# Twenty-four chains of taps in groups of three in the tail's linear attention

## The chip, the core and the metric

The kernel runs on one core of one Trainium2 chip. The core has five engines, each with an instruction queue of its own that it works through in order: PE (TensorE, matrix products), DVE (VectorE), ACT (ScalarE), POOL (GpSimd) and SP (SyncE, which here only issues transfers). Engines wait for each other by semaphores. The metric is the device time of one execution in microseconds (us); smaller is better.

## The reference

Four images of 256 channels and 64 x 64 pixels, float32, go through four layers. Each one normalises its input by groups, computes, and adds its result to what came in:

```python
x = x + layer0(gn(x))   # 1x1 conv, deformable sampling, feed-forward
x = x + layer1(gn(x))   # linear attention
x = x + layer2(gn(x))   # 3x3 convolution with binarised weights
x = x + layer3(gn(x))   # softmax attention over a max-pooled image
```

The change concerns layer 1, and one buffer of layer 2. Layer 1, cut to what matters:

```python
qkv = relu(conv2d(x, qkv_w, 'SAME') * qkv_bn_scale + qkv_bn_bias)  # 768 channels
agg = conv2d(qkv, agg_dw_w, [(2, 2), (2, 2)], groups=C3) + agg_dw_b  # 5x5, each channel alone
agg = conv2d(agg, agg_pw_w, 'SAME', groups=C3) + agg_pw_b            # one factor per channel
ms = concatenate([qkv, agg], axis=1)                                 # 64 heads of 24 channels
q, k, v = split(ms.reshape(B, -1, 24, H * W), 3, axis=2); q = relu(q); k = relu(k)
vk = einsum('bhdn,bhen->bhde', v, k)
out = einsum('bhde,bhen->bhdn', vk, q)
denom = einsum('bhe,bhen->bhn', k.sum(-1), q)
out = relu(bn(conv2d(out / (denom + EPS), proj_w)))
```

The 5 x 5 convolution of each channel by itself is what the "taps" are: 25 products with a factor per channel, summed, for each of 768 channels and 4096 pixels.

## The kernel before

A tile of work holds 128 channels (the partitions) by pixels. The 768 channels of qkv are six such tiles, two each of q, k and v. An image is cut into eight blocks of 512 pixels (NB), and for the taps into four pieces of 16 rows, 1024 pixels (NCH). So one image needs 6 x 4 = 24 **chains of taps**, each of 25 instructions of 128 x 1024 elements.

Layers overlap between images. Generators hand out work piece by piece, each piece with a cost, and `beside` advances several of them by shares of their stated totals. Most of the run is bound by the gathers of layer 0's sampling on GpSimd, with the other layers of earlier images beside it. When the fourth image has been sampled, the **tail** begins (`self.alone` is set in `run`). Its first stage runs three works in the share of 0 to 1: the feed-forward of image 3 (0 to 0.27), the linear attention of image 3 (0.27 to 1, with the total LAST), and layers 2 and 3 of image 2, called `rest` (0.27 to 1.05). The instructions of PE, DVE, ACT and POOL stand in this stage in the order in which the program emits them; SP's do not. The second stage runs layer 2 of image 3, conv(3), beside what is left of `rest`, in an order that a scheduler chooses. Layer 3 of image 3 ends the run.

Linear attention is `layer1`. `rows` produces: for three pairs of tiles, (k, v), (k, v) and (q, q), it multiplies each block by the weights (L824), and ScalarE writes the result into a padded buffer of 20 rows (`pad0` for the first of the pair, `pad1` for the second; `padded` clears the edges with memsets on DVE, L459). In the tail `room(3)` gives each of the two names four buffers. When a piece of 16 rows is complete, it goes to `ready`, and `chains` hands out its two chains in order.

A chain is done in one of two ways. `aggregate` runs it on DVE: `depthwise` multiplies and adds in one instruction per tap, the first at L180, the others at L178, into an accumulator in PSUM. `products` runs it on two engines: ScalarE multiplies a tap into one of three buffers named m (L196), and GpSimd adds that to the sum in SBUF (L200); it takes 28 steps for 25 taps, because its adds trail its products by up to two steps.

Around the taps stands `step`, which is called with `chains=True` once for each tap on DVE in the tail. At every second tap it takes one item from the list `later` and emits it; at count 6 of 8 it advances `rows` once; and it advances the chains on ScalarE and GpSimd. `later` holds the uses of finished chains: the outer products of k and v (`outer`: transposes, a copy on ScalarE, a product), their combination (`summed`), and for the q pieces the `output` (denominators L924, inverse L928 and L929 on DVE, heads, projection L946, residual). They are `staged`: each item holds the next link of up to three or more uses, so that one engine's link is a step ahead of the next engine's.

Nine of the chains (`ASIDE`) run on ScalarE and GpSimd, taken by `others` from the same sequence as DVE takes its own; `due` grows with each tap by `ASIDE * 28 / (6 * NCH - ASIDE) / 25` = 9 x 28 / 15 / 25 = 0.672, and each whole unit advances them by a step. These run across the ends of DVE's chains, independently of them. What is left of them after DVE's fifteenth chain is drained, then what is left in `later`.

Layer 2 is `layer2`. For each of eight blocks `normed` takes a buffer `xp`, clears its edges (DVE, L1049), loads ten rows (SP, L1052) and normalises them (ScalarE, L1053); `parts` forms sums and differences from it (L1041, on GpSimd in the tail), and PE multiplies them (L1090). The results are added to the residual on DVE (L1070 to L1074). In the tail `xp` has two buffers, so the next block can be loaded while the current one is read. Layer 3's softmax takes for each 128 pixels the products L1190, the largest element (DVE, L1191), the exponential (ScalarE, L1196), transposes, and the product L1208.

Of the kernel before, what the change touches and what calls it, by code (L numbers as in the profile page):

```python
# [38 lines left out]

CONVOLVE, OFFSETS, BINARY = NB * 9 + 26, 60, 62  # L40
FEED = NB * 40 + 8
LINEAR, LAST, ASIDE = 938, 592, 9
STEPS = 900
CONV, SECOND = NB * 22.5 + 11, 568
EPS_BN = 1e-5
# [26 lines left out]
class Net:  # L72
# [684 lines left out]
    def layer1(self, n, st, st2):  # L757
# [3 lines left out]
        with tc.tile_pool(name=f"la{n}", bufs=1, side="right") as sp, \  # L761
# [10 lines left out]
            ld = sp.tile([P, 4, 2, 32], F32, name="ld")  # L772
            nc.vector.memset(ld, 0.0)

            later, count, aside, due = [], 0, None, 0
            alone = self.alone
            room = lambda bufs, more=1: bufs + more * alone

            def step(cost, chains=False):


                nonlocal count, due
                count += chains
                if later and (not alone or count % 2 or not chains):
                    later.pop(0)()
                if chains:
                    if count % 8 == 6 if alone else count in LEADS:
                        next(made, None)
                    if aside:
                        due += ASIDE * 28 / (6 * NCH - ASIDE) / 25  # L790
                        while due > 1:
                            next(aside, None)
                            due -= 1
                return cost


# [12 lines left out]
            def rows():  # L809


                for t, tiles in enumerate(((2, 4), (3, 5), (0, 1))):
                    new = lambda c: [self.padded(bp, 1, 20, 2, c, f"pad{i}", bufs=room(3)) for i in range(2)]
                    pads = {0: new(0)}
                    for b in range(NB):
                        c, h = divmod(b, 2)
                        x = self.block(bp, self.x3_d[n], b, "xr")
                        if h and c + 1 < NCH:
                            pads[c + 1] = new(c + 1)
                        got = []  # L820
                        for i, m in enumerate(tiles):
                            ps = self.ps()
                            for k in range(KT):
                                nc.tensor.matmul(ps, qw[:, k, m * P:(m + 1) * P], x[:, k], start=k == 0, stop=k == KT - 1)  # L824
                            if alone:
                                yield
                            bn = {"bias": qb[:, m:m + 1], "scale": self.vec("qkv_s", m)}
                            dst = {j: p[i][:, 0] for j, p in pads.items()}
                            if t < 2:
                                v = bp.tile([P, 512], F32, name="v", tag=f"v{i}")  # L830
                                added = {} if i else {"accum_out": ks[t][:, 0, b:b + 1]}
                                nc.scalar.activation(v, ps, AF.Relu, **bn, **added)
                                self.spread(dst, rw(v), b, 2)
                                got.append(v)
                            else:
                                self.spread(dst, None, b, 2, lambda own: nc.scalar.activation(own, rw(ps), AF.Relu, **bn))  # L836
                            if i:
                                if got:
                                    outer(t, 0, *got, t == 0 and b == 0, False)
                                for j in [c - 1] * (b > 0 and not h) + [c] * (b == NB - 1):  # L840
                                    ready.append((t, tiles, j, [p[:, 0] for p in pads.pop(j)]))
                            if not alone:
                                yield
# [163 lines left out]
                    yield step(3)  # L1007
                return args

            def others():  # L1010

                for _ in range(ASIDE):
                    while not (args := next(every)):
                        yield
                    *args, more = args
                    yield from products(*args, **more)

            if alone:
                aside, number = others(), ASIDE
            while number < 6 * NCH:  # L1020
                count = 0 if not alone and number % 2 == 0 else count
                *args, more = yield from chain()
                yield from aggregate(*args, **more)
                number += 1
            if aside:
                for _ in aside:
                    pass
            while later:
                yield step(2 if alone else 4)

# [1 line left out]
    def layer2(self, n, st, st3, side="left"):  # L1032
# [3 lines left out]
        with tc.tile_pool(name=f"ca{n}", bufs=1, side=side) as sp, \  # L1036
                tc.tile_pool(name=f"cb{n}", bufs=2, side=side) as bp:
            w = sp.tile([P, KT, 3, 4, C], F32, name="w2")
            nc.sync.dma_start(w, self.w2_d)
            sc, bi = yield from self.groupnorm(sp, st, "g2")  # L1040
            add = lambda out, a, b, op=ALU.add: (nc.gpsimd if self.alone else nc.vector).tensor_tensor(out, a, b, op)  # L1041

            def normed(b):

                lo, hi = max(8 * b - 1, 0), min(8 * b + 9, H)
                xp = bp.tile([P, KT, 10, W + 2], F32, name="xp", bufs=1 + self.alone)
                for v in [xp[:, :, :, 0:1], xp[:, :, :, W + 1:]] + [xp[:, :, 0:1, 1:W + 1]] * (b == 0) \
                        + [xp[:, :, 9:10, 1:W + 1]] * (b == NB - 1):
                    nc.vector.memset(v, 0.0)  # L1049
                for k in range(KT):  # L1050
                    v = xp[:, k, lo - 8 * b + 1:hi - 8 * b + 1, 1:W + 1]
                    nc.sync.dma_start(v, self.x4_d[n][:, k, lo * W:hi * W].rearrange("p (r w) -> p r w", w=W))  # L1052
                    nc.scalar.activation(v, v, AF.Identity, bias=bi[:, k:k + 1], scale=sc[:, k:k + 1])  # L1053
                d = xp.rearrange("p k r (x d) -> p k r x d", d=2)
                return [d[:, :, :, c // 2:c // 2 + W // 2, c % 2] for c in range(4)]

            def parts(d):
                v = bp.tile([P, 4, KT, 10, W // 2], F32, name="xd")
                add(v[:, 0], d[0], d[2], ALU.subtract)
                add(v[:, 1], d[1], d[3], ALU.subtract)  # L1060
                yield
                add(v[:, 2], d[1], d[2])
                add(v[:, 3], d[2], d[1], ALU.subtract)
                yield v

            def leave(b, m, half, ps, xv):

                y = xv[:, m].rearrange("p (q d) -> p d q", d=2)
                if not half:
                    nc.vector.tensor_tensor(y, y, ps, ALU.add)  # L1070
                    return
                nc.vector.tensor_tensor(y, y, ps[:, 0:1].to_broadcast([P, 2, 256]), ALU.add)
                nc.vector.tensor_tensor(y[:, 0], y[:, 0], ps[:, 1], ALU.add)
                nc.vector.tensor_tensor(y[:, 1], y[:, 1], ps[:, 1], ALU.subtract)  # L1074
                if m == KT - 1:
                    self.stats(st3, xv, b)
                    nc.sync.dma_start(self.x5_d[n][:, :, b * 512:(b + 1) * 512], xv)

            before, made = [], []
            for d in parts(normed(0)):  # L1080
                yield 2
            for b in range(NB):
                v, xv = d, self.block(bp, self.x4_d[n], b, "x4")
                ahead = iter(())
                for m in range(KT):
                    for half in range(2):
                        ps = self.long().rearrange("p (e q) -> p e q", e=2)
                        for i in range(12):
                            e, k, t = i // 6, i // 3 % 2, i % 3
                            nc.tensor.matmul(ps[:, e], w[:, k, t, 2 * half + e, m * P:(m + 1) * P], v[:, 2 * half + e, k, t:t + 8],  # L1090
                                             start=i % 6 == 0, stop=i % 6 == 5)
                            if i % 3 == 2:
                                if before and (i > 5 or not self.alone):
                                    before.pop()()
                                if i == 5 and b + 1 < NB:
                                    if not (m or half):
                                        ahead = parts(normed(b + 1))
                                    elif half:
                                        d = next(ahead)
                                yield 1.4  # L1100
                        before.append(partial(leave, b, m, half, ps, xv))
            before.pop()()
# [286 lines left out]
```

## Time and profile before

| | us |
|---|---|
| median of 3 runs | 8705.34 |
| lowest and highest | 8691.91, 8707.14 |
| the profiled execution | 8769.03 |
| its span | 8767.3 |
| the tail, from the end of the gathers | about 1577 (7190 to 8767) |
| first to last tap on DVE in the tail | 702.4 (7551.6 to 8254.0) |

Durations below come from the profiled execution, which took 0.7% longer than the median. Over its whole span the engines were busy as follows (us and share, then the number of instructions):

```profile
PE 5927.3 (68%) x35776; PEld 3524.6 (40%) x35776; DVE 4790.2 (55%) x6020; ACT 3564.8 (41%) x10792; POOL 4995.0 (57%) x4894
```

In the table of slices each digit is the busy share of a fortieth of the span, 219 us, in tenths:

```profile
DVE  5344442443366667324776675127766762588723
ACT  2333333234433433344444443444444442456414
POOL 2666666556666666666665556666655560487410
```

The tail is the last seven digits. The chains of taps lie in the sixth- to third-last of them. A row of the table of groups reads: line, engine, operation, output and inputs, shapes, number, then busy us and mean ns of one, then the idle time of the engine just before them and what ended it.

### The profile page before, as it was taken

To read this page: it belongs to the slowest core of one execution; us is meant where nothing else is said; L and a number is where in the kernel's file an instruction comes from. 1 tells how busy PE (TensorE), PEld (TensorE's weight loads), DVE (VectorE), ACT (ScalarE), POOL (GpSimd) and SP (SyncE) were. 2 spreads that over 40 slices of the span, in tenths; PEclk is the share of its full clock that TensorE was granted. 3 is DMA by queue.
4 is the path that set the end of the run, shared out by engine and by line. 5 is a ranking of instruction groups with operands and counts; after the bars stand their busy time and mean duration, and the time that the engine had idled before them with its cause. 6 is when DMAs were issued, how large, how long until landed. Compare 5 with 4: busy or idle time off the path is not lost.

```text
span 8767.3 us, 99783 instructions
## 1 busy us (share of the span) xinstructions
PE 5927.3 (68%) x35776; PEld 3524.6 (40%) x35776; DVE 4790.2 (55%) x6020; ACT 3564.8 (41%) x10792; POOL 4995.0 (57%) x4894
## 2 busy tenths in 40 slices
PE   4454554448744546688876676888766768987899
PEld 2222222223322322335644443345544433664476
DVE  5344442443366667324776675127766762588723
ACT  2333333234433433344444443444444442456414
POOL 2666666556666666666665556666655560487410
PEclk7666666669866667799987787999878879987899
DMA  6454554454433334444443344444433342220131
GB/s 171 129 157 123 144 150 117 119 146 142 153 107 108 105 109 125 135 130 141 135 133 106 110 115 141 141 133 139 139 105 109 111 118 95 77 68 30 44 96 53
DMA packets 744383, 1031.75 MB, mean 118 GB/s; under 512 B 354128, under 2 KB 459984, under 8 KB 742352
## 3 DMA queue, kind: packets, MB, share of 16 engines
q0 software_dynamic: 221184, 604.27, 24.1%
q1 hardware_dynamic: 522704, 421.10, 16.3%
q8 instruction: 283, 4.64, 0.2%
q14 instruction: 212, 1.74, 0.1%
HBM read 856.39 MB, written 168.61 MB: 117 GB/s over the span
## 4 chain that ended last, share of the span: by engine, by line
PE 42%; another core or an unknown queue 18%; DVE 16%; ACT 13%; issue 8%; POOL 2%; DMA 1%; SPq 0%; ACTq 0%; DVEq 0%; POOLq 0%
DVE agg L178 9%; PE acc L603 6%; PE ps L739 5%; ACT wm L588 5%; PE ps L1090 5%; PE ps L749 5%; PE ps L824 3%; PE ps L946 2%; PE ps L1208 2%; PE s L1190 2%; PE po L636 2%; ACT dT L623 2%; ACT at L608 1%; POOL av L200 1%
## 5 line engine op out<-in xcount | busy, mean ns | idle before, releaser
L596 POOL DMA_INDIRECT g<-tab,sl x4608 | 4401.8, 955 | 2848.3 <-issue 1184.1
L178 DVE SCALAR_TENSOR_TENSOR agg<-pad,vec,agg 128x1024 f32<-128x1024 f32 x2257 | 2904.0, 1287 | 63.3
L603 PE MATMUL acc<-g,wm 128*32 128x128 f32 x18432 | 1018.1, 339 | 2033.0 <-ACT at L608 1573.1
L603 PEld LDWEIGHTS acc<-g,wm 128*32 128x32 f32 x18432 | 562.9, 130 | 2532.2 <-ACT at L608 1785.6
L588 ACT ACTIVATE wm<-sl,con 128x48 f32<-128x48 f32 x6144 | 1486.9, 364 | 25.5 <-remote 12.0
L1090 PE MATMUL ps<-xd,w 128*128 128x256 f32 x3072 | 745.9, 395 | 28.6 <-issue 19.1
L623 ACT COPY dT<-dp 64x128 f32<-64x128 f32 x1152 | 296.3, 257 | 972.9 <-remote 475.5
L1090 PEld LDWEIGHTS ps<-xd,w 128*128 128x128 f32 x3072 | 594.4, 199 | 144.4 <-issue 61.1
L608 ACT COPY at<-acc 128x256 f32<-128x256 f32 x576 | 214.4, 372 | 774.5 <-remote 670.6
L739 PE MATMUL ps<-x2f,f 128*128 128x512 f32 x1024 | 506.6, 643 | 11.8 <-DVE hm L724 7.7
L824 PE MATMUL ps<-xr,qw 128*128 128x512 f32 x768 | 469.2, 741 | 19.5 <-issue 7.4
L724 DVE SCALAR_TENSOR_TENSOR hm<-ps,vec,lk 128x512 f32<-128x512 f32 x256 | 190.6, 749 | 518.7 <-ACT lk L741 391.6
L749 PE MATMUL ps<-hm,f 128*128 128x512 f32 x1024 | 463.5, 601 | 0.0
L200 POOL TENSOR_TENSOR av<-av,m 128x1024 f32<-128x1024 f32 x144 | 342.9, 2382 | 110.8 <-ACT m L196 102.0
L741 ACT ACTIVATE lk<-ps,low 128x512 f32<-128x512 f32 x256 | 174.3, 687 | 529.2 <-PE ps L739 401.5
L1041 POOL TENSOR_TENSOR xd<-xp 128x640 f32<-128x640 f32 x64 | 79.5, 1270 | 522.7 <-ACT xp L1053 421.9
L878 ACT COPY kt<-pt 128x512 f32<-128x512 f32 x256 | 149.2, 583 | 532.5 <-remote 255.6
L636 PE MATMUL po<-dT,ow 128*128 128x288 f32 x1024 | 328.7, 468 | 49.5 <-issue 14.1
L1208 PE MATMUL ps<-gt,pT 128*128 128x129 f32 x2048 | 316.8, 316 | 44.2 <-ACT pT L1204 34.8
L613 PE MATMUL dp<-ident,at 128*128 128x128 f32 x1152 | 288.2, 340 | 83.0 <-ACT dT L623 55.6
L1208 PEld LDWEIGHTS ps<-gt,pT 128*128 128x128 f32 x2048 | 299.1, 227 | 96.4 <-ACT pT L1204 45.8
L1190 PE MATMUL s<-ph,th 128*128 128x512 f32 x512 | 287.6, 673 | 46.0 <-ACT pad L836 12.6
(243 smaller groups left out, 7700.2 us busy)
## 6 DMA issues: line engine op xcount, KB each, us to landing
g<-tab,sl POOLq DMA_INDIRECT x4608
x<-x SPq DMA_DIRECT2D x128, 512.0 KB
xr<-x SPq DMA_DIRECT2D x96, 512.0 KB
tab<-xo SPq DMA_DIRECT2D x192, 128.0 KB
x<-in_x SPq DMA_DIRECT2D x32, 512.0 KB
y<-yc SPq DMA_DIRECT2D x32, 512.0 KB
yb<-y SPq DMA_DIRECT2D x64, 256.0 KB
x<-yb SPq DMA_DIRECT2D x64, 256.0 KB
```

Of the source, the lines that this page charges most:

```text
L178: nc.vector.scalar_tensor_tensor(to, s, wt, acc, ALU.mult, ALU.add)
L588: nc.scalar.activation(wm[:, :, :, o], blocks[b][:, r:r + WR, G:], AF.Copy, scale=self.con("own")[:, o:o + 1])
L596: nc.gpsimd.indirect_dma_start(out=g[:, i, :], out_offset=None, in_=table, in_offset=bass.IndirectOffsetOnAxis(ap=sl.bitcast(I32)[:, r, i: ...
L603: nc.tensor.matmul(acc[32 * i:32 * i + 32, :], wm[:, r4, 4 * i + 2 * x:4 * i + 2 * x + 2, :], g[:, i, x * P:(x + 1) * P], start=x == 0, st ...
L623: nc.scalar.copy(dT[b][hs, :, r:r + UR], dp[u][hs, :, :, s, :].rearrange("p v g o -> p g v o"))
L636: nc.tensor.matmul(po[m][:, 0:BR * OB], self.ow[:, k, m * P:(m + 1) * P], dT[b][:, k].rearrange("p r o -> p (r o)"), start=k == 0, stop=k ...
L739: nc.tensor.matmul(ps, f1[:, k, m * P:(m + 1) * P], x2[:, k], start=k == 0, stop=k == KT - 1)
L749: nc.tensor.matmul(ps, f2[:, k, m * P:(m + 1) * P], hm[:, k], start=k == 0, stop=k == 4 * KT - 1)
L824: nc.tensor.matmul(ps, qw[:, k, m * P:(m + 1) * P], x[:, k], start=k == 0, stop=k == KT - 1)
L1090: nc.tensor.matmul(ps[:, e], w[:, k, t, 2 * half + e, m * P:(m + 1) * P], v[:, 2 * half + e, k, t:t + 8], start=i % 6 == 0, stop=i % 6 == 5)
L1190: nc.tensor.matmul(s[i], tv[:, 4 * b + j], ph[:, i * 512:(i + 1) * 512], start=True, stop=True)
L1208: nc.tensor.matmul(ps[:, 0:P + 1], pT[:, m], gt[:, m], start=m == 0, stop=m == 7)
```

## The change

The fixed number ASIDE and the running count `due` go. In the tail the loop now takes three chains at a time: the first goes to DVE; the second, `slow`, to ScalarE and GpSimd; then the third to DVE. Every second tap of the two DVE chains (an odd `count`) advances the slow one by one step; after the third chain what is left of the slow one is drained. Eight such groups make 16 chains on DVE and 8 on ScalarE and GpSimd, in the place of 15 and 9. The total LAST, by which `beside` paces the layer, becomes 624. In the tail `pad1` gets a fifth buffer, and `xp` of layer 2 has one buffer in the place of two, in both stages of the tail. The staging of the uses stays as it is, and nothing changes ahead of the tail.

```diff
-LINEAR, LAST, ASIDE = 938, 592, 9
+LINEAR, LAST = 938, 624
...
-            later, count, aside, due = [], 0, None, 0
+            later, count, aside = [], 0, None
...
-                    if aside:
-                        due += ASIDE * 28 / (6 * NCH - ASIDE) / 25
-                        while due > 1:
-                            next(aside, None)
-                            due -= 1
+                    if count % 2 and aside:
+                        next(aside, None)
...
-                    new = lambda c: [self.padded(bp, 1, 20, 2, c, f"pad{i}", bufs=room(3)) for i in range(2)]
+                    new = lambda c: [self.padded(bp, 1, 20, 2, c, f"pad{i}", bufs=room(3) + (alone and i)) for i in range(2)]
...
-            def others():
-
-                for _ in range(ASIDE):
-                    while not (args := next(every)):
-                        yield
-                    *args, more = args
-                    yield from products(*args, **more)
-
-            if alone:
-                aside, number = others(), ASIDE
             while number < 6 * NCH:
                 count = 0 if not alone and number % 2 == 0 else count
                 *args, more = yield from chain()
-                yield from aggregate(*args, **more)
-                number += 1
-            if aside:
-                for _ in aside:
-                    pass
+                if alone:
+
+                    *slow, smore = yield from chain()
+                    aside = products(*slow, **smore)
+                    yield from aggregate(*args, **more)
+                    *args, more = yield from chain()
+                    yield from aggregate(*args, **more)
+                    for _ in aside:
+                        pass
+                    number += 3
+                else:
+                    yield from aggregate(*args, **more)
+                    number += 1
...
-                xp = bp.tile([P, KT, 10, W + 2], F32, name="xp", bufs=1 + self.alone)
+                xp = bp.tile([P, KT, 10, W + 2], F32, name="xp", bufs=1)
```

More of the change, by code (lines that the diff above doesn't have):

```diff
@@ L779, in step @@
             def step(cost, chains=False):
-                nonlocal count, due
+                nonlocal count
                 count += chains
```

## The prediction

> **What bounds the kernel now.** I read the page's slices first: the tail, from about 7190 us, has no gathers on GpSimd (POOL) any more, and the digit of DVE rises to 8. Then I cut the tail into windows by what runs there, and read busy time in each (the columns are window, its length, busy us and instructions of PE, PEld, DVE, ACT and POOL, granted clock, DMA share, GB/s).
>
> ```profile
> 7551.00:7815.00 264.00, 242.87 (x1165) 196.02 (x1163) 232.97 (x273) 170.44 (x228) 237.30 (x113) 0.98 0.23 68
> 7815.00:8254.00 439.00, 321.08 (x1154) 195.12 (x1154) 397.60 (x442) 267.85 (x369) 308.23 (x129) 0.80 0.13 41
> 8254.00:8358.00 104.00, 93.07 (x321) 50.57 (x320) 43.01 (x69) 30.51 (x50) 0.00 (x0) 0.89 0.16 54
> 8358.00:8520.00 162.00, 155.66 (x714) 134.17 (x715) 46.10 (x112) 28.14 (x38) 39.55 (x32) 0.95 0.38 112
> ```
>
> The first two rows are the chains of taps beside the binarised convolution of image 2, then beside its softmax: DVE is 88% and 91% busy, 630.6 of 703 us. The third is the drain, the outputs that are left after the last tap, where PE is 89% busy. The fourth, conv(3), is PE at 96%. Next, the groups of the window of the chains, and what DVE waits for in it (us in total, times, longest).
>
> ```profile
> L178 DVE SCALAR_TENSOR_TENSOR agg<-pad,vec,agg 128x1024 f32<-128x1024 f32 x345 | 443.3, 1285 | 8.3
> L200 POOL TENSOR_TENSOR av<-av,m 128x1024 f32<-128x1024 f32 x144 | 342.9, 2382 | 110.8 <-ACT m L196 102.0
> L200 POOL TENSOR_TENSOR ak<-ak,m 128x1024 f32<-128x1024 f32 x72 | 171.3, 2379 | 41.6 <-ACT m L196 37.0
> L1041 POOL TENSOR_TENSOR xd<-xp 128x640 f32<-128x640 f32 x26 | 32.5, 1272 | 0.0
> L196 ACT ACTIVATE m<-pad,vec 128x1024 f32<-128x1024 f32 x216 | 246.6, 1158 | 63.0 <-POOL av L200 43.7 <-POOL ak L200 19.0
> ```
> ```profile
> DVE rden L1211 <- PE ps L1208: 10.7, 5, 4.9
> DVE x L1072 <- PE ps L1090: 10.4, 2, 7.6
> DVE mx L1191 <- PE s L1190: 9.6, 9, 3.7
> DVE pad L459 <- ACT m L196: 9.2, 1, 9.2
> ```
>
> Taps alone are 443.3 us of DVE here. Its longest wait inside the chains is the 9.2 us of L459: the memset of a fourth pad buffer stood until ScalarE had read the old contents. All DVE waits over 0.3 us between first and last tap come to 58 us. Last, the chain of waits from 7551 to 8358 goes through the taps most, but through GpSimd's adds for 22.8%:
>
> ```profile
> by line: DVE agg L178 19.2%; POOL av L200 14.8%; POOL ak L200 5.9%; PE ps L1208 5.5%; issue 4.9%; PE ps L946 4.5%; PE ps L824 4.0%; ACT m L196 3.9%; PE s L1190 3.1%; PE rden L937 3.1%; DVE mx L1191 3.0%; PE ps L1090 2.3%; POOL xd L1041 2.1%
> ```
>
> So the stretch is bound by DVE's work, with GpSimd close to it in the first window (237.3 of 264 us).
>
> **What the Trainium skill says.** "Perfetto Trace Analysis", Optimization Strategy: take each regime's most contended engine and find the gaps on it and what ends them; a repeating gap can mean too few buffers. Here the regime is DVE's, its gaps are 8% of the stretch, and only the 9.2 us is one of buffers. "GPSIMD Engine Reference", 3.1 Elementwise, puts a float32 add on GpSimd at about twice VectorE's time; the trace agrees: 2.38 us for an add against 1.285 us for a tap (1.85 times), so two taps last a little longer than one add. Section 8, Key points, of the same page: the two engines share SBUF interfaces and contend when a VectorE instruction has two SBUF inputs. A tap has one (its accumulator lies in PSUM), and its mean is 1285 ns beside GpSimd's adds and 1287 ns over the whole kernel, so I charge nothing for contention.
>
> **The change, part by part.** The sum is made against the profiled execution (8769.03 us, span 8767.3); the median of 8705.34 us lies 0.7% lower, and the difference is carried over to it unscaled.
>
> *Which chains run where.* Before, 15 chains run on DVE and 9 on ScalarE and GpSimd; after, 16 and 8. DVE gains one chain: 24 taps x 1.285 = 30.8 us, and one first tap (L180) of 1.35 us, its row's mean. In the emitted order of after, the reciprocal of one more output, L928 and L929, comes ahead of the last tap: 0.69 + 3.35 = 4.0 us by the timeline at 8254 us. That makes +36.2 us of DVE between first and last tap (645.6 before, 681.9 after, by the same durations). ScalarE loses 27 activations of 1.158 us and GpSimd 24 adds of 2.38 us. Both wait in these windows already (POOL 152 us for ScalarE), so their gain is worth nothing by itself.
>
> *The pacing.* Before, the slow side makes 0.67 step for each tap and runs by itself, over chains' ends; after, one step for each second tap, and what is left is drained at each group's end (three steps, two adds). Two taps and the DVE work between them take 2 x 1.70 = 3.4 us against 2.38 for an add, so GpSimd keeps up. Before, GpSimd is saturated from its first add at 7569 us to 7815 us (237.3 of 246 us), and ScalarE waits 63 us for it in the whole stretch, behind which evictions for PE stand. That gets better. What it gives to DVE is bounded by DVE's waits that are not the buffer's, nor a PE result of its own in the softmax: nothing to 40 us. I take 3, because waits for rden, mx and r (24.5 us) come at the end of PE chains of their own.
>
> *The fifth buffer of pad1.* In the emitted order of after each pad memset has at least 13 taps between the old buffer's last reader and itself; 9.2 us of wait go (bounds 5 to 9.2).
>
> *One xp buffer in the place of two.* Each block's memset on DVE and load on SP now follow the last GpSimd subtraction of the block before. From the end of the adds to both halves normalised takes 6 to 8 us in conv(3)'s blocks; the next adds are due later than that in most blocks. Behind the memset stand taps, behind the normalisation on ScalarE stand m and evictions. I lay before's own times over it and get waits of 3.5 and 1.5 us on two of the memsets of conv(2): +2 after what the eased GpSimd queue returns (bounds 0 and 10; priced again as a rival). In conv(3), PE needs 20.7 us per block and the adds 4.95 us, so reload of 6 to 8 us fits: 0 (bounds -3 and +5). SP's loads are issued later, with nothing of length queued behind them.
>
> *The end of the stretch.* 34 staged items stand in the queue after the last tap, before 38. 104 us / 38 = 2.7 us each, so -11 us; but one softmax iteration that stood beside them goes to the stage after, which is PE-bound, for about +6. Net -5 (bounds -15 and 0). LAST 624 makes the linear layer end at 0.983 of the stage instead of 0.999, and image 2's work stands at the same place then (531.7 units both), so this changes little: 0.
>
> Sum: 36.2 - 9.2 - 3 + 2 - 5 + 0 = +21 us, 8790 us in the profiled execution, 8726 on the median.
>
> **The rivals.**
> *A (this forecast).* The sixteenth chain is paid, most else is small: +8 to +36 us by the bounds that are likely together, 8713 to 8741. For it: DVE at 90%, and its waits in the second window end on PE. Against it: the chain of waits leaves DVE for half its length.
> *B, waits pay it back.* The eased ScalarE and GpSimd queues remove some 25 us of the 58 instead of 3: 21 - 22 = -1, 8704; with a smaller share +15, 8720. For it: 63 us of ScalarE waiting for GpSimd, and 14 us of DVE waiting for L1090 in the first window. Against it: PE has 92% in that window by itself.
> *C, the other side.* GpSimd, saturated from 7569 to 7815, sets the pace of ScalarE, PE and DVE through the one queue. With 24 adds for 50 taps it falls out, and DVE's waits shrink to 12 us: 681.9 + 12 = 694 against 702.4, -8 us, and -11 in the drain with nothing given back: -19, 8686. It decides from about 40 us of waits that vanish. For it: 22.8% of the chain of waits in these adds. Against it: ScalarE's waits mostly stand ahead of further m, which no one else reads.
> *D, the single xp buffer is late.* The reload joins the chain adds, load, normalise, adds in conv(2), and DVE stands at the memset about 4 us in each of seven blocks: 21 + 28 = +49, 8754. For it: DVE's order is fixed, so a late memset holds taps. Against it: GpSimd had run ahead by a block.
>
> **How the numbers follow.** Chances: A 0.52, B 0.28, C 0.11, D 0.09. About 0.2%, 17 us, is what a measurement of this kernel tells from no change. A lies over it with 0.46 and under it with 0.06; D is slower; B is within (0.28); C is faster. So faster 0.11, same 0.34, slower 0.55. The range 8690 to 8750 holds A and B, half of C's spread and half of D's. A's own is 8713 to 8741.
>
> **What would show it.** First to last tap: about 727 us instead of 702; if under 705, B or C. L178 in the stretch 24 more, L200 192. No wait at L459 over 3 us; a wait of L1049 for POOL's L1041 repeated over blocks shows D. POOL in the first window well under 90%, and ScalarE's wait for POOL below 30 us; if those fall and DVE's waits for PE stay, A's reason is right. From last tap to conv(3)'s first statistics 95 to 104 us. The forecast is wrong if DVE's waits in the stretch fall below 25 us or rise over 75.

## The result and the profile after

| | before | after |
|---|---|---|
| median of 21 runs each, us | 8711.85 | 8692.57 |
| lowest and highest, us | 8689.68, 8728.44 | 8665.56, 8729.88 |
| ratio, with its 95% interval | | 0.9983 (0.9973 to 0.9993) |
| profiled execution, its span, us | 8769.03, 8767.3 | 8695.07, 8693.3 |

The changed kernel is faster by 0.17%, 15 us (6 to 24) by the ratio and 19 us by the medians, where 21 us slower had been forecast. The two spans differ by 74 us, but most of that lies in code that is the same in both kernels: the last gather ends at 7251.4 us before and at 7191.1 us after. So the comparison is made by stages of the tail, cut at the first and the last tap on DVE and at the first group statistics of conv(3) (L117). Inside the taps, the part beside the convolution ends where DVE starts to wait for the statistics of image 2's softmax layer (L117 as well). Each kernel was profiled once more among the experiments (e3, e4); both values are given.

| stage, us | before | after | difference of the means |
|---|---|---|---|
| last gather to first tap | 300.2, 298.5 | 293.8, 297.6 | -3.7 |
| first to last tap | 702.4, 699.3 | 711.2, 710.0 | +9.8 |
| of it, DVE busy | 641.7, 639.6 | 671.3, 672.1 | +31.1 |
| of it, DVE idle, beside the convolution | 24.1, 24.1 | 13.5, 10.6 | -12.1 |
| of it, DVE idle, beside the softmax | 36.7, 35.6 | 26.3, 27.3 | -9.4 |
| drain: last tap to conv(3)'s statistics | 104.0, 103.9 | 85.0, 85.0 | -19.0 |
| statistics to the end | 409.3, 409.0 | 412.2, 411.4 | +2.7 |

"Idle" is here the sum of DVE's gaps over 0.05 us, "busy" the rest of the stretch. So the shorter gaps, 11 to 12 us, count as busy, and the views below, which count covered time alone, give less (659.3 us after, 630.6 before). The stages repeat within some 4 us, the drain within 0.1; the first row differs by no more than that. The sixteenth chain is paid: DVE is 31 us more busy. But waits of 21.5 us, two thirds of it, are gone, and the drain is 19 us shorter. The rows add up to a tail that is 10 us shorter, within the interval of the ratio. These are the rows of the changed kernel that answer to those shown of before (window, length, busy us and instructions of PE, PEld, DVE, ACT, POOL, granted clock, DMA share, GB/s):

```profile
7484.90:7744.00 259.10, 245.25 (x1159) 195.77 (x1157) 238.79 (x274) 159.60 (x224) 209.66 (x102) 0.97 0.25 70
7744.00:8196.00 452.00, 319.81 (x1170) 190.13 (x1171) 420.52 (x469) 250.15 (x348) 278.69 (x117) 0.81 0.13 42
8196.00:8281.00 85.00, 80.28 (x296) 44.78 (x295) 35.75 (x62) 25.68 (x42) 0.00 (x0) 0.96 0.15 50
8281.00:8443.00 162.00, 155.36 (x712) 132.66 (x713) 49.61 (x117) 32.40 (x45) 36.97 (x30) 0.96 0.38 113
```

GpSimd has left its limit in the first window (81% busy, before 90%), DVE has risen to 92 and 93%, and the drain has 25 fewer records of matrix products at a higher clock, 0.96 against 0.89. Next the groups of the changed kernel from first to last tap. The reader is to see the end of the row L196: ScalarE waited 63.0 us for GpSimd before, now 5.2.

```profile
L178 DVE SCALAR_TENSOR_TENSOR agg<-pad,vec,agg 128x1024 f32<-128x1024 f32 x368 | 473.2, 1286 | 8.9
L200 POOL TENSOR_TENSOR av<-av,m 128x1024 f32<-128x1024 f32 x96 | 228.3, 2378 | 102.0 <-ACT m L196 97.1
L200 POOL TENSOR_TENSOR ak<-ak,m 128x1024 f32<-128x1024 f32 x96 | 228.1, 2376 | 120.5 <-ACT m L196 116.1
L1036 POOL TENSOR_TENSOR xd<-xp 128x640 f32<-128x640 f32 x28 | 35.0, 1270 | 6.6 <-ACT xp L1048 6.6
L196 ACT ACTIVATE m<-pad,vec 128x1024 f32<-128x1024 f32 x192 | 219.4, 1160 | 5.2 <-POOL av L200 5.2
```

What DVE waits for in the same window (lines from `aggregate` on stand three to five lower here than before: L1206 is the former L1211, L1067 the former L1072):

```profile
DVE mx L1186 <- PE s L1185: 9.2, 13, 1.7
DVE x L1065 <- PE ps L1085: 8.3, 1, 8.3
DVE agg L180 <- ACT pad L470: 8.1, 1, 8.1
DVE x L1067 <- PE ps L1085: 5.0, 2, 3.2
DVE rden L1206 <- PE ps L1203: 3.0, 3, 1.4
```

No memset waits any more, neither L459 (9.2 us before) nor L1044; rden fell from 10.7 to 3.0 us. These two make up most of what went: 9.2 of the 12.1 us beside the convolution, 7.7 of the 9.4 us beside the softmax. The waits for PE beside the convolution (L1065, L1067) stayed, 13.3 us against 14.4 before. The wait of L180 belongs to the very first tap and lies outside the stretch. And the chain of waits to the end of the drain goes through DVE's taps for 38.2% now, before for 19.2%; GpSimd's adds, 22.8% of it before as the sum of L200 and L1041, have one entry of 2.2% among those listed (the list is cut at its end):

```profile
by line: DVE agg L178 38.2%; issue 4.9%; PE ps L821 4.6%; PE ps L943 4.4%; PE s L1185 4.4%; PE ps L1085 3.3%; PE ps L1203 3.1%; DVE mx L1186 2.9%; POOL ak L200 2.2%; PE rden L934 2.2%; PE ps L1213 1.7%; DVE rd L926 1.7%; DVE st L110 1.5%; D
```

### The profile page after: what moved, and what is told of

Its sections match the earlier page's. It is cut to its first block, busy times and chain, and to the rows that moved or that the text cites. A ratio compares the mean times of both kernels' runs of the same rounds, so it can differ in the third digit from the quotient of the medians.

```text
span 8693.3 us, 99761 instructions
## 1 busy us (share of the span) xinstructions
PE 5880.0 (68%) x35776; PEld 3498.6 (40%) x35776; DVE 4817.7 (55%) x6045; ACT 3541.0 (41%) x10767; POOL 4934.7 (57%) x4870
## 4 chain that ended last, share of the span: by engine, by line
PE 43%; another core or an unknown queue 17%; DVE 17%; ACT 13%; issue 8%; DMA 1%; POOL 0%; SPq 0%; ACTq 0%; DVEq 0%; POOLq 0%
DVE agg L178 10%; PE acc L603 6%; PE ps L739 5%; PE ps L749 5%; ACT wm L588 5%; PE ps L1085 4%; PE ps L821 3%; PE ps L943 2%; PE ps L1203 2%; PE s L1185 2%; PE po L636 2%; ACT dT L623 2%; ACT at L608 1%; PE rden L934 1%
## 5 line engine op out<-in xcount | busy, mean ns | idle before, releaser
L178 DVE SCALAR_TENSOR_TENSOR agg<-pad,vec,agg 128x1024 f32<-128x1024 f32 x2280 | 2934.5, 1287 | 63.9
L739 PE MATMUL ps<-x2f,f 128*128 128x512 f32 x1024 | 502.3, 639 | 10.2 <-issue 5.1
L821 PE MATMUL ps<-xr,qw 128*128 128x512 f32 x768 | 463.5, 733 | 21.8 <-issue 8.5
L613 PE MATMUL dp<-ident,at 128*128 128x128 f32 x1152 | 285.5, 336 | 77.1 <-ACT dT L623 53.4
L739 PEld LDWEIGHTS ps<-x2f,f 128*128 128x128 f32 x1024 | 199.2, 203 | 253.3 <-issue 238.5
```

Of the source, the lines that this page charges most:

```text
L178: nc.vector.scalar_tensor_tensor(to, s, wt, acc, ALU.mult, ALU.add)
L739: nc.tensor.matmul(ps, f1[:, k, m * P:(m + 1) * P], x2[:, k], start=k == 0, stop=k == KT - 1)
```

## The experiments

Chips differ in the whole time (the kernel before took 8777, 7742, 8771 and 8770 us in the four sets of runs), so only ratios to the kernel before on the same chip, and stages of the profiles, are compared. The stages carry over between chips: e7, on the chip of 7742 us as e5, e6 and e8 are, is the kernel before up to the drain, and its stretch is that of e3 to the tenth. The stages of all runs:

| run | first to last tap | DVE busy | idle, conv. and softmax | drain | ratio (95%) |
|---|---|---|---|---|---|
| e1 buffers alone | 699.6 | 641.2 | 21.8 + 36.5 | 103.7 | 0.9996 (0.9987 to 1.0004) |
| e2 split, free pacing | 710.8 | 672.0 | 10.7 + 28.1 | 96.4 | 0.9999 (0.9989 to 1.0009) |
| e3 before again | 699.3 | 639.6 | 24.1 + 35.6 | 103.9 | one run |
| e4 after again | 710.0 | 672.1 | 10.6 + 27.3 | 85.0 | one run |
| e5 before, half adds | 664.9 | 619.3 | 12.1 + 33.6 | 97.0 | one run |
| e6 after, half adds | 700.2 | 657.0 | 10.6 + 32.6 | 83.9 | one run |
| e7 before, PE filled | 699.3 | 639.6 | 24.1 + 35.6 | 100.2 | one run |
| e8 two paces | 698.6 | 640.0 | 14.1 + 44.4 | 104.5 | 0.9998 (0.9989 to 1.0006) |
| e9 after, no pairs | 684.6 | 649.0 | 10.6 + 25.0 | 85.2 | 0.9960 (0.9946 to 0.9973) |
| e10 before, no pairs | 680.5 | 618.9 | 24.1 + 37.5 | 98.2 | 0.9977 (0.9969 to 0.9984) |
| e11 before, earlier uses | 707.1 | 645.8 | 24.1 + 37.2 | 88.5 | one run |
| e12 after, all | 688.4 | 651.2 | 10.6 + 26.6 | 77.7 | 0.9970 (0.9959 to 0.9982) |

**e1 and e2: the change taken apart.** e1 has the buffers alone, e2 the buffers and the split of 16 and 8 chains, but not the groups:

```diff
-                    new = lambda c: [self.padded(bp, 1, 20, 2, c, f"pad{i}", bufs=room(3)) for i in range(2)]
+                    new = lambda c: [self.padded(bp, 1, 20, 2, c, f"pad{i}", bufs=room(3) + (alone and i)) for i in range(2)]
-                xp = bp.tile([P, KT, 10, W + 2], F32, name="xp", bufs=1 + self.alone)
+                xp = bp.tile([P, KT, 10, W + 2], F32, name="xp", bufs=1)
```
```diff
-LINEAR, LAST, ASIDE = 938, 592, 9
+LINEAR, LAST, ASIDE = 938, 624, 8
```

> The kernel before with only the two buffer edits: pad1 five buffers in the tail, xp one. 15 and 9 chains and their pacing stay. Theory Q (ScalarE's queue: what helps is that GpSimd no longer saturates and ScalarE no longer waits for it): the 9 us wait of the pad memset goes, ScalarE still waits about 60 us for GpSimd, first to last tap 693 to 700 us (702 before), ratio 0.999 to 1.0005. Rival F (the fifth buffer alone makes the gain): first to last tap under 690 us, ratio 0.998 or less. Rival X (one xp buffer costs): first to last tap over 703 us, waits of L1049 for GpSimd repeated over the blocks.

> The kernel before with the buffer edits and ASIDE 8 and LAST 624: 16 and 8 chains as in the changed kernel, but the slow ones still run by their count (0.56 step a tap), across the ends of DVE's chains, not in groups of three. Theory Q: the lighter load on GpSimd is what counts, not the groups: ScalarE waits under 20 us for GpSimd, first to last tap 705 to 718 us, drain (last tap to conv(3)'s statistics) 84 to 95 us, ratio 0.997 to 0.9995. Rival S (running in step is what counts): ScalarE waits over 30 us, first to last tap over 720 us, ratio 1.001 or more.

The buffers alone are worth nothing that the ratio could tell, and little in the stretch: DVE's idle time beside the convolution is 21.8 us in e1 and 24.1 in e3. The waits on DVE of e1 in that part tell why:

```profile
DVE x L1072 <- PE ps L1090: 8.8, 2, 7.6
DVE xp L1049 <- POOL xd L1041: 8.7, 3, 4.0
DVE x L1070 <- PE ps L1090: 4.0, 1, 4.0
```

The pad's wait of 9.2 us has gone, and the one xp buffer has put 8.7 us in its place, waiting for a full GpSimd. In e2, where GpSimd has eight chains, both are gone: idle 10.7 us, ScalarE waiting 26.3 us for GpSimd in the whole stretch, and a stretch of 710.8 us, the same as with groups (711.2, 710.0). So the waits that come back in the stretch come with the split; the groups take ScalarE's wait further down, from 26 to 5 us, and the stretch has nothing of it. What the groups bring is in the drain: 96.4 us in e2, 85.0 after. This is e2's row of it:

```profile
8272.70:8369.10 96.40, 87.96 (x302) 47.17 (x300) 36.06 (x63) 26.89 (x46) 0.00 (x0) 0.90 0.13 44
```

PE's clock is about as low in it as before, 0.90 against 0.89. e2's ratio, 0.9999, came out above the range that theory Q had for it, and its drain over the 84 to 95 us. So the split and the buffers without the groups are no gain: a stretch 10 us longer eats up a drain 7.6 us shorter. The changed kernel is faster by what its drain has beyond that.

**e3 and e4: the two kernels again.** The same kernels, with no edit.

> The kernel before once more, for the spread of a profile's stages. If the stages carry the difference: first to last tap 702 plus or minus 4 us, drain 104 plus or minus 4, the tail from the last gather 1516 plus or minus 6. If the drain of 104 us was an accident of that profile (granted clock 0.89 in it): 90 to 98 us.

> The changed kernel once more. If the stages carry the difference: first to last tap 711 plus or minus 4 us, drain 85 plus or minus 4, the tail 1502 plus or minus 6. If the short drain was an accident (granted clock 0.96 in it): 90 to 100 us.

The drain repeats within 0.1 us, its granted clock too (0.89 and 0.96): it is no accident of one profile.

**e5 and e6: GpSimd's load taken away.** In either kernel GpSimd's adds leave out the lower half of the rows:

```diff
-                nc.gpsimd.tensor_tensor(acc, acc, made[t - 1], ALU.add)
+                nc.gpsimd.tensor_tensor(acc[:, :rows // 2], acc[:, :rows // 2], made[t - 1][:, :rows // 2], ALU.add)
```

> The kernel before, with each of GpSimd's adds of the slow chains over the upper 8 of 16 rows only (half of these sums is left out), so GpSimd is never full and ScalarE never waits for it; nothing else moves. Theory Q (DVE's waits fell because GpSimd is no longer full, through ScalarE's queue): DVE's idle time from first to last tap falls from 60 to about 40 us, the stretch to 678 to 684 us. Rival R (the waits fell because one chain more on DVE fills the time in which it waited for PE, whatever GpSimd does): the stretch stays at 696 to 702 us with 56 to 60 us idle. Under both the drain stays at 104 us.

> The changed kernel with the same half of the adds left out. Theory Q: GpSimd was not in the way any more, the stretch stays at 708 to 712 us and the drain at 85. If GpSimd still held something: under 704 us.

ScalarE's wait for GpSimd in e5 is 2.5 us, and DVE's idle time beside the convolution falls from 24.1 to 12.1 us, where the changed kernel has it, with no chain moved and no buffer added: theory Q holds there. First what DVE still waits for in that part of e5, then the wait for rden beside the softmax:

```profile
DVE x L1072 <- PE ps L1090: 7.6, 1, 7.6
DVE x L1070 <- PE ps L1090: 4.0, 1, 4.0
```
```profile
DVE rden L1211 <- PE ps L1208: 9.9, 5, 4.7
```

The memset's wait of 9.2 us has gone without a fifth pad buffer. Beside the softmax, idle time falls by 2 or 3 us only, of the 9 that the change brought, and the wait for rden, which fell to 3.0 us in the changed kernel, stays at 9.9 us, so GpSimd's load isn't what it hangs on. With the sixteenth chain but without the groups (e2) it is 7.0 us. Rival R is left for part of it, and no run tests it by itself. Three other figures missed. The drain of e5 fell to 97.0 us, where 104 had been expected (see e7). The stretch of e5 went to 664.9 us, not 680, and that of e6 to 700.2, not 708 to 712. DVE itself was 20 us (e5) and 15 us (e6) less busy, with the same instructions. The taps kept their 1.285 us; other rows did not. First a row of before, then the same row of e5:

```profile
L1155 DVE TENSOR_TENSOR xq<-m 128x256 f32<-128x256 f32 x8 | 11.6, 1444 | 0.3
```
```profile
L1155 DVE TENSOR_TENSOR xq<-m 128x256 f32<-128x256 f32 x8 | 4.4, 545 | 0.3
```

The timeline of before shows how this comes about, first DVE, then GpSimd (start, duration, and a number of instructions joined in one line):

```profile
7838.16 1.98 DVE L1152 TENSOR_TENSOR m<-x 128x512 f32<-128x512 f32 x1
7838.24 0.07 DVE L1142 MEMSET gt<- 128x8 f32 x1
7840.17 2.47 DVE L1155 TENSOR_TENSOR xq<-m 128x256 f32<-128x256 f32 x1
7842.56 2.60 DVE L178 SCALAR_TENSOR_TENSOR agg<-pad,vec,agg 128x1024 f32<-128x1024 f32 x2
7845.07 2.81 DVE L1152 TENSOR_TENSOR m<-x 128x512 f32<-128x512 f32 x1
7847.91 2.44 DVE L1155 TENSOR_TENSOR xq<-m 128x256 f32<-128x256 f32 x1
```
```profile
7834.79 17.77 POOL L200 TENSOR_TENSOR av<-av,m 128x1024 f32<-128x1024 f32 x7 [5.71 <-ACT m L196]
```

The two operations have two inputs in SBUF, though not two tiles, as the expectation of e9 says: the maximum takes two views of one tile. Inside the run of seven adds they take 1.98 to 2.81 us; with GpSimd idle, the same two lines take 0.69 and 0.42 us at 7858 us. In the stretch of before, each one that met an add ended 0.55 us (512 elements) or 0.28 us (256) after the end of that add: it stood until the add was done. The 24 operations of L1152, L1155 and L954 take 31 to 34 us per stretch, in both kernels, in place of the 14 us that 8 x (0.69 + 0.42 + 0.68) would give. An addition of the same shape with one input in PSUM (L1070) stays at 0.68 us in the part where GpSimd is 90% busy:

```profile
L1070 DVE TENSOR_TENSOR x<-x,ps 128x512 f32<-128x512 f32 x16 | 10.9, 682 | 4.0 <-PE ps L1090 4.0
L954 DVE TENSOR_TENSOR xq<-xq,pr 128x512 f32<-128x512 f32 x8 | 10.6, 1328 | 0.0
```

A few operations with one tile and a factor per channel stood as well: two of L908 and one of L1128 in before took 1.99 to 2.36 us, where the others of their kind take 0.22 to 0.27, and ended less than 0.1 us after an add.

**e7: the clock in the drain.** One edit gives PE something to do while it would wait for the third output's inverse:

```diff
                             nc.tensor.matmul(pd[0][32 * j:32 * j + 32], ld[:, j, h], qh[h][j], start=h == 0, stop=h == 1)
+                    if alone and c == 2:
+                        fill = self.ps("fill")
+                        for _ in range(6):
+                            nc.tensor.matmul(fill, pw[:, 0, 0:P], fl(aq[0])[:, 0:512], start=True, stop=True)
```

> The kernel before with six products of 128x512 added after the denominators of the third output, in which PE otherwise stands still for about 2 us just after the last tap; their result is read by nobody. Theory K (the drain is long because TensorE's clock is halved for 14 us after that idle moment, which falls into the drain before and ahead of it in the changed kernel): no half clock in the first 25 us of the drain, granted clock over 0.94, drain 97 to 101 us in spite of 4 us more work. Rival L (the clock's dips fall where they will; the drain is a matter of items and their order): clock 0.89, drain 107 to 109 us.

The rows around the last tap (at 8254 us) of before, then of e7 (at 7216 us):

```profile
8256.00:8260.00 4.00, 2.16 (x8) 1.15 (x7) 2.24 (x2) 0.37 (x1) 0.00 (x0) 1.00 0.17 65
8260.00:8274.00 14.00, 14.00 (x34) 7.06 (x32) 4.25 (x7) 2.44 (x4) 0.00 (x0) 0.52 0.00 1
8274.00:8284.00 10.00, 10.00 (x24) 4.42 (x23) 3.65 (x7) 2.41 (x4) 0.00 (x0) 1.00 0.00 0
```
```profile
7218.00:7222.00 4.00, 4.00 (x13) 1.86 (x12) 2.54 (x1) 0.00 (x0) 0.00 (x0) 1.00 0.34 123
7222.00:7236.00 14.00, 13.30 (x58) 7.63 (x57) 5.19 (x10) 3.76 (x7) 0.00 (x0) 1.00 0.00 0
```

Before, PE works 2.16 of 4 us just after the last tap, and then runs at half clock for 14 us (0.52), all of them busy. In e7 it is kept busy, and the clock stays at 1.00: 58 products in the 14 us that held 34. The drain is 3.7 us shorter with 12 matrix-product records more in it (333 against 321). Up to the last tap its clock goes as in before (0.83 and 0.92 in the two stretches of 20 us ahead of it, in both), so it is the filling that kept it up. Theory K holds for what the dip costs and for what prevents it here. But the idle moment alone doesn't bring the dip. e5, which nothing fills, has the same moment (its last tap is at 7182 us):

```profile
7184.00:7188.00 4.00, 2.16 (x9) 1.19 (x8) 2.30 (x2) 0.37 (x1) 0.00 (x0) 1.00 0.27 97
7188.00:7202.00 14.00, 13.30 (x46) 6.81 (x45) 5.02 (x9) 3.40 (x6) 0.00 (x0) 1.00 0.00 0
```

PE works 2.16 of 4 us there too, and the clock stays at 1.00. With the same 321 records the drain took 97.0 us, 7 less than before: that is about the price of the dip. What else decides whether it comes stays open. In the changed kernel such a dip exists too, but earlier:

```profile
8182.00:8188.00 6.00, 0.59 (x2) 0.00 (x0) 5.93 (x4) 0.00 (x0) 0.84 (x1) 0.83 0.03 11
8188.00:8198.00 10.00, 8.36 (x23) 4.99 (x24) 9.12 (x12) 4.75 (x7) 4.70 (x2) 0.50 0.01 2
8198.00:8208.00 10.00, 10.00 (x26) 4.90 (x26) 3.64 (x7) 1.63 (x3) 0.00 (x0) 0.92 0.00 0
```

It falls nearly all before the last tap (at 8196 us), where DVE, 9.12 of 10 us busy, sets the pace and half a clock on PE should cost little. Nothing in the change aims at this place; e2, with the same split, still has the low clock in its drain.

**e8: two paces for nine slow chains.**

```diff
-                        due += ASIDE * 28 / (6 * NCH - ASIDE) / 25
+                        due += 0.6 if number < ASIDE + 5 else 0.73
```

> 15 and 9 chains as before, with the changed kernel's buffers, but two paces for the slow chains: 0.60 step a tap for DVE's first five chains, beside the convolution that uses GpSimd too, 0.73 after. If theory Q is right and GpSimd's fullness beside the convolution is what counts: ScalarE waits under 35 us for GpSimd (63 before), the stretch 685 to 695 us, ratio 0.997 to 0.999. If the total load of nine chains is what counts: ScalarE waits 50 us or more, the stretch 697 to 703, ratio 1.000.

The run has the buffers of e1 as well. Beside the convolution it did what theory Q says: idle 14.1 us, near the 12.1 of e5. But the adds put off came due beside the softmax, where idle rose from 35.6 to 44.4 us, and ScalarE's wait was 48.1 us, between the two forecasts. The stretch came to 698.6 us and the time stayed the same. Moving GpSimd's work later in this way is no gain; of the two readings, the one by the total of nine chains fits.

**e11: uses taken earlier.**

```diff
-                if later and (not alone or count % 2 or not chains):
+                if later and (not alone or count % 2 or not chains or count > 366):
```

> The kernel before, but during the last nine taps an item of the uses is taken at each tap, not at each second one, so that 34 are left after the last tap, as in the changed kernel, and not 38. Theory D (the drain is as long as what is left in the list): the drain falls from 104 to 90 to 96 us, the stretch grows by 2 to 5. Rival K' (the drain's length lies in the clock's dip alone): the drain stays within 4 us of 104 if the granted clock stays at 0.89.

The drain fell to 88.5 us, more than theory D had, the stretch grew by 5 to 8 us. The clock rose to 0.95 with it; the third output's inverse now stands ahead of the last tap (8240.6 us, the last tap ends at 8247.1). The row of the drain:

```profile
8247.10:8335.60 88.50, 83.20 (x311) 45.92 (x310) 36.50 (x64) 28.41 (x47) 0.00 (x0) 0.95 0.15 50
```

Against before, PE's busy time times its clock is 4 us less, its time without work 6 us, and what the low clock took 6 us: the work that left is the smaller part. The tail of this run, 1503.6 us from the last gather, is as short as that of the changed kernel (1502.2, 1504.0), with 15 and 9 chains and one line changed. Its one time, 8746.8 us, lies just below the lowest of 30 runs of the kernel before on that chip (8747.8). So neither the split nor the groups are needed for a tail this short.

**e9, e10 and e12: a version that beats both.** The max pool becomes one reduction with a single input, in all images, and in the tail GpSimd does the residual add of three of four output pieces:

```diff
-                m1 = bp.tile([P, KT, 256], F32, name="m1", tag="pe")
-                v = x.rearrange("p k (x d) -> p k x d", d=2)
-                nc.vector.tensor_tensor(m1, v[:, :, :, 0], v[:, :, :, 1], ALU.max)
...
+                nc.vector.tensor_reduce(xq.rearrange("p k (r x) -> p (k r) x", x=W // 2),
+                                        x.rearrange("p k (r d x e) -> p (k r) x d e", d=2, e=2, x=W // 2), AX.XY, ALU.max)
...
-                    nc.vector.tensor_tensor(x[:, m], x[:, m], pr[h, m], ALU.add)
+                    (nc.gpsimd if alone and c < 3 else nc.vector).tensor_tensor(x[:, m], x[:, m], pr[h, m], ALU.add)
```

> The changed kernel without most VectorE operations that read two tiles in SBUF beside GpSimd's adds: the max pool of layer 3 as one reduction over 2 x 2 that reads one tile (8 and 8 operations of 1.37 and 1.46 us in the stretch become 8), and the residual add of the first three output pieces on GpSimd. Theory P (such operations stand still while a GpSimd add runs; the half-adds run took 0.45 to 0.9 us off each): a reduction takes 1.1 to 1.3 us, DVE is 20 us less busy from first to last tap, the stretch 688 to 696 us, ratio to the kernel before 0.995 to 0.9975. Rival (DVE's waits for PE grow by what it saves): stretch over 702 us, ratio about 0.998 as without this edit.

> The kernel before with the same two edits. Theory P: DVE is 22 to 26 us less busy from first to last tap, because GpSimd runs more of the time here; but GpSimd is full beside the convolution, so idle stays 55 to 62 us; the stretch 674 to 684 us, ratio 0.9965 to 0.9985. If the contention explains the part of the change's gain in DVE's busy time, the difference of the stretch to the run of the changed kernel with these edits is 12 to 16 us in place of 10.

In e9 from first to last tap:

```profile
L951 POOL TENSOR_TENSOR xq<-xq,pr 128x512 f32<-128x512 f32 x8 | 10.2, 1280 | 13.1 <-ACT pr L947 13.1
L1146 DVE TENSOR_REDUCE xq<-x 128x256 f32<-128x1024 f32 x8 | 9.7, 1211 | 0.0
```

A reduction of 1.21 us stands where two operations took 1.31 + 1.44 us in the changed kernel. Away from GpSimd's adds the two took 0.69 + 0.42 = 1.11 us, so the reduction isn't faster in itself: it doesn't stand. DVE is 23 us less busy in e9, 22 in e10, and its idle time stays within 4 us: both stretches fall, to 684.6 and 680.5 us. In e9 some 12 us of it are the max pool's; the rest is the residual adds, of which 8 x 0.68 = 5.4 us are work moved to GpSimd. Theory P holds, for e9 with a stretch below its range. The difference of the two stretches, 4.1 us, is not the 12 to 16 that I had expected: the two-input operations cost both kernels about as much, so that contention isn't what made the change faster. e10's drain is 6 us shorter as well, at a clock of 0.96. e9 is the best version here, 0.9960 of the kernel before. The changed kernel had 0.9983 on another chip, and the two intervals just touch; e9's tail of 1472.7 us is some 30 us shorter.

e12 adds the edit of e11 to e9 (`count > 391`).

> The changed kernel without the two-tile operations (as e9) and with an item of the uses taken at each of the last nine taps (as e11), 29 items left after the last tap in place of 34. If the gains add: drain 72 to 78 us (85 in e9), stretch 688 to 693 (685 in e9), ratio to the kernel before 0.9945 to 0.996. If PE is the limit of both by now: drain and stretch together stay within 3 us of e9's 770.

Drain and stretch together went from 769.8 to 766.1 us, but what follows took 413.8 us, before 409.7, and the ratio of 0.9970, on another chip, is no better than e9's. What the drain lost came back after it: the gains don't add.

## Why the prediction was wrong

Its direction was wrong: the change itself went the other way. That the median lies in the range on record, at its lower edge, comes from a range that was made to hold rival B as well. In the profiles the tail is 10 us shorter where +21 was forecast, a miss of 31 us: 11 at the end of the stretch, 11 in the waits, 5 in DVE's work, and 4 ahead of the first tap, no more than that stage varies by itself. By its steps:

- **"Which chains run where", +36.2 us of DVE**: measured +31.1. The taps and the inverse came as counted, +32.4 and +4.0 us (a chain's last tap, which writes to SBUF, stands in another row, so the row of L178 has 23 more and not 24). Some 6 us were given back by small operations that no longer stood for GpSimd's adds: L124 and L126 2.5 us, L1128 2.1, L908 1.7. The 645.6 us that this step names as DVE's work before are in no view; only the difference enters the sum.
- **"So I charge nothing for contention"**: right for taps, wrong as a rule for the engine. I had the sentence of the Trainium skill, "GPSIMD Engine Reference", Key points, and tested it on the one operation that it doesn't concern. In e5, with adds of half the rows, DVE was 20 us less busy in the stretch. It hardly decided the sign, since both kernels pay about as much, but hid the best edit of the case.
- **"The fifth buffer of pad1", -9.2 us**: the wait went as told, but the buffer with the single xp is worth little by itself (e1), and in e5 the wait went with four buffers. What it hung on was the full GpSimd. The buffer is paid by xp's second one, and xp's waits (8.7 us in e1) vanish only with the lighter GpSimd. The two terms should have been one.
- **"One xp buffer", +2**: 0 with 8 slow chains. Rival D didn't occur.
- **"The pacing", "I take 3"**: this term failed in the stretch. Idle time fell by 21.5 us together; the forecast had 10.2 net, of which 9.2 through the buffer. Beside the convolution 12.1 us went, by GpSimd's fullness, as e5 shows. Beside the softmax 9.4 us went, most of it the wait for rden, of which the prediction said that it comes at the end of a PE chain of its own. e5 gives 2 or 3 of these 9 us to GpSimd; what the wait for rden hung on stays open. The chosen value sat at the bottom of bounds (0 to 40) that held the result.
- **"The end of the stretch", -5, bounds -15 and 0**: measured -19.0 in the drain and +2.7 after it, -16.3 together, outside its bounds. PE's busy time times its granted clock went from 93.07 x 0.89 = 82.8 to 80.28 x 0.96 = 77.1 us (-5.7, the work that left). PE's time without work went from 10.9 to 4.7 us (-6.2), and what half clock took went from 10.2 to 3.2 us (-7.0). I had sized only the items, at -11, and put the other two terms at nothing without a reason. The clock of 0.89 stood in the third row that I showed; I read the 89% of PE's busy time in it and passed over the clock. The +6 us after the drain came out as 2.7.
- **conv(3), 0**: with all that follows, the +2.7 already counted, within the bounds given for conv(3).

Of the rivals, B came nearest in the stretch: waits paid back about 21 of 31 us. C had the sign, by the wrong road: the stretch grew by 10 us where C let it shrink by 8, and the drain gave more than all. And the sign is in part luck. Some 7 us of the drain, nearly half of what was gained in the whole, depend on where a dip of the clock falls, which no forecast and no part of the change aimed at. Of the signs named, GpSimd's share (81%) and ScalarE's wait (5.2 us) fell as asked. The stretch (711 and 710 us) fell between its two marks, and DVE's waits of 38 to 40 us stayed inside the 25 to 75; the drain of 85 us, not 95 to 104, was the one that spoke.

## What to carry to other kernels

When work moves off an engine that is full, look at what stands in the queue of the engine that feeds it: here, with a ninth of GpSimd's chains taken away, the waits fell by two thirds of the price of one more chain on the engine that bounds the stretch, and about 14 of these 21 us fall with GpSimd's load alone (e5). Multiply busy time by granted clock before calling a stage bound by matrix products: an idle moment just ahead of such a stage can cost more than it lasts, though it need not (e7, e5). And on VectorE, look for rows whose mean is twice that of equal shapes elsewhere; beside a busy GpSimd, a form with one input can be worth more than a better schedule. Before a gain is put down to a change of schedule, try a one-line shift of the last uses: here it gave a tail as short (e11).

## What the runs showed of the hardware

- A VectorE operation with two inputs in SBUF doesn't run slower beside a GpSimd add, it waits for that add's end: 2.47 us for one of 128x256 that takes 0.42 us alone, and even 2.19 us for one of 128x2. With one input in PSUM it doesn't wait (128x512: 0.68 us throughout), nor does the reduction of e9 (1.21 us); a few operations with one tile and a factor per channel did (L908, L1128: about 2 us in place of 0.2). The Trainium skill, "GPSIMD Engine Reference", Key points, names this contention without a price.
- TensorE's clock halved for about 14 us after some 2 us without work, and stayed at full when that moment was filled (e7). It stayed at full with the moment left as it was, too (e5), so such a moment alone is not enough. "TensorE: Matmul & The Clock Gate", What's actually happening, says that throttled is the default and that activity releases it; the run with the filling agrees. e5, at full clock without the filling, leaves open when the clock drops. That PE, busy for 14.00 of 14 us, ran at half clock all that time before release I had not expected.
